# A four-layer graph stack: block sums copied by ScalarE in the third layer, projections taken before the factors

## The chip, the cores and the metric

The kernel runs on one core of a Trainium2 chip. The metric is device time in microseconds for one execution; the median of three executions is given for the kernel before. The core has a matrix engine (TensorE, PE in the profile; its weight loads are PEld), a vector engine (VectorE, DVE), an activation engine (ScalarE, ACT), a general engine (GpSimd, POOL) and a queue engine that issues transfers (SyncE, SP). Each takes its own instructions in order and waits for the others by semaphores. PE writes its products into PSUM, eight banks of 128 x 512 float32; all else is kept in SBUF. GpSimd works on SBUF only in this kernel.

## The reference

Four graph layers follow each other on x (4096 x 256, float32) with one adjacency matrix (4096 x 4096, integers). After each, the input is added and every row is normalised. The change touches the third layer and the start of the fourth:

```python
# layer 2 (the third)
h = x @ W
e = (h @ a[:D, 0])[:, None] + (h @ a[D:, 0])[None, :]
e = jnp.where(e > 0, e, NEG_SLOPE * e)
attention = jax.nn.softmax(jnp.where(adj > 0, e, MASK_VAL), axis=1)
x = _layernorm(x + jax.nn.elu(attention @ h))
...
# layer 3 (the fourth)
Qn, Kn = _cos_normalize(x @ Wq.T), _cos_normalize(x @ Wk.T)
att = jax.nn.softmax(jnp.where(adj > 0, Kn @ Qn.T, NEG), axis=1)
x = _layernorm(x + 0.5 * (att @ x) + 0.5 * x)      # rows without a neighbour keep x
```

The exponential of the third layer's leaky sum splits into a part by source and a part by target, so the attention weight is a maximum of two products of factors, times the mask.

## The kernel before

**Tiling.** Rows are cut into 8 blocks (b) of 512. Within a block the 4096 neighbours are taken in 16 units (g) of 256. The third layer is `additive_one`. For every unit `weights` loads a mask (L552, SP), has ScalarE write two tiles of factors `r` (L564, into two PSUM banks) and VectorE turn each into attention weights, `prob` (L565, which reads one `r` and the mask). For blocks after the first, the product is done with seven half-sized multiplications in place of eight: `mix_weights` makes four combined tiles, the first two in one VectorE instruction (L434), the others by GpSimd (L435, L436). `prob` and `mix` have four buffers each.

**Sums.** `sums` runs a unit's seven products (`product`, L444), which add into four banks, `acc` 0 to 3, over the whole block. There is one set of these banks. At the end of a block the four banks are joined into the tile `quarters`: ScalarE copies half a bank to `one` (L449), VectorE adds the rest in two parts, `first_half` (L450, L452, L453) and `second_half` (L457, L458). The first block uses two banks and needs copies only (L587 to L589).

**Order.** The loop runs over all 128 units of the layer with a lag of three: in one step it issues the weights of unit i and the sums of unit i - 3, and then one step of finishing the block before. The code fixes the order of PE, VectorE and ScalarE as written; GpSimd and the transfers are placed by the scheduler. In the text, g=5 means the step that issues the sums of unit 5, and with it the weights of unit 8. When g is 15, the sums and the joining are issued ahead of the weights.

**Finishing a block.** `finish` projects the joined sums of the block before (`project`, L594, in steps g = 1, 2, 4, 6, into two banks `g`), and takes each projection: `take` has VectorE make the reciprocal of the weights' sum (L600) and ScalarE make `e` and `h` from it (L602, L603). `add` (L611, L612, L154, L155 on VectorE) adds the input, in steps 3, 4, 6, 8. `dots` (L502 on VectorE) and `sources` (L515 and a transfer on ScalarE, with unit 8) prepare the next block's factors. Before, `dots` wrote its products into one of the buffers of `h`.

**The fourth layer's preparation.** From the third block on, `follow.prepare` works ahead for the fourth layer, one step at a time: transposes (L127), a transfer out, four transfers back, sixteen multiplications (L1059), squares (L1066), scaled rows (L1075), and a second turn by transposes and transfers. The fourth layer itself is `cosine_attention`: scores (L1115) into two banks `p` or, for some, into the banks `g`, exponentials (L1119), masks (L1127), and the same `product`. `tail` finishes the third layer's last block inside it.

**PSUM.** Each layer opens its pools in turn. The third has `r` (2 banks), `acc` (4), `g` (2), in this order. The fourth had `acc` (4), `p` (2), `g` (2), so `p` stood on the last two banks of the third layer's `acc`.

Of the kernel before, what the change touches and what calls it, by code (L numbers as in the profile page):

```python
# [9 lines left out]
FP = mybir.dt.float32  # L10
# [4 lines left out]
OP = mybir.AluOpType  # L15
AX = mybir.AxisListType
PSUM = bass.MemoryType.PSUM

P = 128
D = 256  # L20
KC = D // P
QB = 4
QW = QB * P
# [5 lines left out]
def kernel(  # L29
# [27 lines left out]
    nc = tc.nc  # L57
    N = x.shape[0]
    NT = N // P
    NB = N // QW  # L60

    def pool(stack, name, bufs, **kw):
        return stack.enter_context(tc.tile_pool(name=name, bufs=bufs, reuse_waits="tile", **kw))
# [4 lines left out]
    fin1 = ctx.enter_context(tc.tile_pool(name="fin1", bufs=1))  # L68
# [352 lines left out]
    NP = NT // 2  # L421
    HW = QW // 2
# [24 lines left out]
    def first_half(c, one, acc):  # L447

        nc.scalar.copy(one, acc[3][:, :HW])  # L449
        nc.vector.tensor_tensor(c[:, :2, :], one.unsqueeze(1).to_broadcast([P, 2, HW]),  # L450
                                acc[0].rearrange("p (h i) -> p h i", h=2), OP.add)
        nc.vector.tensor_tensor(c[:, 2, :], c[:, 1, :], acc[1][:, :HW], OP.add)  # L452
        nc.vector.tensor_tensor(c[:, 3, :], c[:, 2, :], acc[1][:, HW:], OP.add)  # L453

    def second_half(c, acc):

        nc.vector.tensor_tensor(c[:, 1:3, :], c[:, 1:3, :], acc[2][:, :HW].unsqueeze(1).to_broadcast([P, 2, HW]), OP.add)  # L457
        nc.vector.tensor_tensor(c[:, 1, :], c[:, 1, :], acc[2][:, HW:], OP.add)  # L458

    def quarters(c, k):  # L460

        lo = k % 2 * P
        return [c[:, q, lo:lo + P] for q in ((0, 3), (1, 2))[k // 2]]
# [61 lines left out]
    def additive_one(w_sb, ga, tail, op, follow):  # L525

        with ExitStack() as lay:
# [4 lines left out]
            sb = pool(lay, "gb_sb", 2)  # L532
# [9 lines left out]
            mixed, acc, prob, mix, mvs, roots, kept, drawn, ys, far_y = {}, {}, {}, {}, {}, {}, {}, {}, {}, {}  # L542
# [4 lines left out]
            def weights(b, g):  # L547
                if b == 0 and g < 2:
                    mask = ga.first_mask[:, 2 * g:2 * g + 2, :]
                else:  # L550
                    mask = mp.tile([P, 2, QW], I32, name="mask")
                    nc.sync.dma_start(mask, edges[:, 2 * g:2 * g + 2, b * QW:(b + 1) * QW])  # L552
                if b < NB - 1:
                    if 4 <= g < 4 + QB:
                        ga.dots((b + 1) * QB + g - 4, (0,), sb, "h")
                    elif g == 8:
                        ga.sources(b + 1)
                    elif g == 11:
                        ga.row(b + 1, nc.sync)
                z = prob[b, g] = zp.tile([P, 2, QW], FP, name="prob")  # L560
                for n in range(2):
                    j = 2 * g + n
                    r = pr.tile([P, QW], FP, name="r")
                    nc.scalar.activation(r, ga.row_of(b), AF.Relu, bias=ga.less[:, j:j + 1], scale=ga.dst[:, j:j + 1])  # L564
                    nc.vector.scalar_tensor_tensor(z[:, n, :], r, ga.own[:, j:j + 1], mask[:, n, :], OP.add, OP.mult)  # L565
                if b:
                    s = mix[b, g] = zp.tile([P, 4, HW], FP, name="mix")
                    mix_weights(s, z, nc.gpsimd)

            def sums(b, g):  # L570
                if g == 0:
                    acc[b] = [pa.tile([P, QW], FP, name=f"acc{n}") for n in range(4)]
                if b:
                    for n in range(7):
                        product(acc[b], prob[b, g], mix[b, g], mixed[g // 2][:, g % 2], g, n)
                else:
                    for j in range(2 * g, 2 * g + 2):
                        for c in range(KC):
                            nc.tensor.matmul(acc[b][c], X[:, j, c * P:(c + 1) * P], prob[b, g][:, j % 2, :],
                                             start=(j == 0), stop=(j == NT - 1))  # L580
                if g == NP - 1:
                    c = kept[b] = op.tile([P, 4, HW], FP, name="quarters")
                    if b:
                        first_half(c, op.tile([P, HW], FP, name="one"), acc[b])
                        second_half(c, acc[b])
                    else:
                        nc.scalar.copy(c[:, :2, :], acc[b][0].rearrange("p (h i) -> p h i", h=2))  # L587
                        nc.vector.tensor_copy(c[:, 3, :], acc[b][1][:, :HW])
                        nc.vector.tensor_copy(c[:, 2, :], acc[b][1][:, HW:])  # L589

            def project(bank, b, k):
                po = drawn[b, k] = bank()
# [3 lines left out]
            def take(sb, b, k):  # L596

                po = drawn[b, k]
                rden = fin.tile([P, 1], FP, name="rden1")
                nc.vector.reciprocal(rden, po[:, D:D + 1])  # L600
                e, h = drawn[b, k] = sb.tile([P, D], FP, name="e"), sb.tile([P, D], FP, name="h")
                nc.scalar.activation(e, po[:, :D], AF.Exp, scale=rden)  # L602
                nc.scalar.activation(h, po[:, :D], AF.Relu, scale=rden)  # L603
# [11 lines left out]
            def finish(b, g):  # L615


                if g in (1, 2, 4, 6):
                    project(bank, b, g // 2)
                if g in (2, 3, 5, 7):  # L620
                    take(sb, b, g // 2 if g > 2 else 0)
                if g in (3, 4, 6, 8):
                    add(b, g // 2 - 1)
                elif g == 10:
                    roots[b] = begin_root(mvs[b])
                elif g == 11:
                    v, r, n = roots[b]
                    end_root(v, r, n, nc.gpsimd)
                    nc.gpsimd.tensor_tensor(v, mvs[b][:, :, 0], r, OP.mult)
                    nc.gpsimd.tensor_scalar(v, v, -1.0, 1.0, OP.mult, OP.add)  # L630
                elif g in (12, 13):
                    v, r, _ = roots[b]
                    for k in (2 * g - 24, 2 * g - 23):
                        y = ys[b][:, k, :]
                        nc.scalar.activation(y, y, AF.Identity, bias=v[:, k:k + 1], scale=r[:, k:k + 1])
                elif g == 14:
                    if b < NB - 2:
                        far_y[b] = saved.tile([P, QB, D], FP, name=f"far_y{b}")
                        nc.scalar.dma_start(far_y[b], ys[b])
                    else:  # L640
                        nc.scalar.dma_start(X[:, b * QB:(b + 1) * QB, :D], ys[b])
# [5 lines left out]
            with tc.manual_schedule(engines=fixed):  # L647
                for i in range(len(units) + LAG):
                    b, g = units[i - LAG] if i >= LAG else (-1, 0)
                    if g == NP - 1:  # L650
                        sums(b, g)
                    if i < len(units):
                        weights(*units[i])
                    if b >= 0:
                        if g < NP - 1:
                            sums(b, g)
                        if b:
                            finish(b - 1, g)
                        else:
                            for _ in range(3 if g > 3 else 0):  # L660
                                next(before, None)
                            if g == 11:
                                follow.start()
                            elif g == 14:
                                follow.centre(bank())
                            if g % 2:
                                t = mixed[g // 2] = keep.tile([P, 2, 4, P], FP, name=f"mixed{g // 2}")
                                mix_features(t, g // 2)
                        if b > 1 and g in (2, 4, 6, 8, 9, 10, 11, 12, 13, 14, 15):
                            follow.prepare(bank, b - 2, 1, ys[b - 2])  # L670
                        if b == NB - 1 and g > 3 and g % 2 == 0:
                            q = g // 2 - 2
                            nc.scalar.dma_start(X[:, q * QB:(q + 1) * QB, :D], far_y[q])
                        if b == NB - 1 and g in (3, 5, 7):
                            follow.load_mask(0, (g - 3) // 2, prob[b, g][:, 0, :1])
# [411 lines left out]
    def cosine_attention(co, tail):  # L1087
# [4 lines left out]
        with ExitStack() as lay:  # L1092
# [4 lines left out]
            far = pool(lay, "co_turn_far", 2, space=bass.MemoryType.DRAM)  # L1097
            co.turning = pool(lay, "co_turn", 1), None, far

            pa = pool(lay, "co_pa", 1, space=PSUM)  # L1100
            pz = pool(lay, "co_pz", 2, space=PSUM)
            ps = pool(lay, "co_ps", 2, space=PSUM)
            ov = out.rearrange("(t p) d -> p t d", p=P)
            mixed, acc, prob, mix, y, back = {}, {}, {}, {}, {}, {}
# [257 lines left out]
```

## Time and profile before

| what | value |
|---|---|
| median of three executions | 2815.4 us (2812.61 to 2818.65) |
| execution profiled | 2813.03 us |
| its span | 2811.2 us, mean granted clock of TensorE 0.998 |
| PE busy | 2776.7 us, 99% of the span |
| DVE busy | 2285.6 us, 81% |
| ACT busy | 1694.8 us, 60% |
| POOL busy | 1049.9 us, 37% |

A busy share is the time in which at least one instruction of an engine was under way, over the span. Matmuls overlap, and their ends are modelled, so a PE that is busy throughout need not be at its peak.

By stages, the third layer's seven blocks that use `mix` lie between 1773 and 2172 us. In these 399.0 us PE is busy for 386.85, DVE for 328.96, ACT for 228.19 and POOL for 197.04. A block from the third on lasts about 58.2 us, from one joining of sums to the next.

How the views are read: the table of waits has a line for each pair of waiting group and releaser, with the total in us, the number of waits and the longest. The timeline has the start, the duration of the merged instructions, the engine, the line, the tiles, and in square brackets the idle time ahead of it and its releaser. The chain of waits follows the last instruction back, each time to what released it, and shows the pieces by start and length. A releaser is inferred: it is the semaphore event that came last, and may not be the one that mattered.

### The profile page before, as it was taken

What the parts mean: (1) busy time and instruction counts of PE and PEld (TensorE: products, weight loads), DVE (VectorE), ACT (ScalarE), POOL (GpSimd) and SP (SyncE); (2) the same over time, 40 slices, a digit from 0 to 9 for tenths busy, and PEclk for the clock granted to TensorE, in tenths of its full rate; (3) what the DMA queues carried; (4) which work ended last, traced back from release to release, by engine and by line L of the source; (5) the groups of instructions that cost most, each with busy time, mean ns of one, the idle gap of its engine ahead of it and who ended that gap; (6) DMA issues with size and microseconds to landing.
All of it is one profiled execution on the core that took longest, in us unless ns stands there. A gap on an engine that the chain in (4) does not pass through costs nothing. (4 is left out here: it accounts for less than half of the span.)

```text
span 2811.2 us, 50179 instructions
## 1 busy us (share of the span) xinstructions
PE 2776.7 (99%) x19449; PEld 1427.4 (51%) x19449; DVE 2285.6 (81%) x3048; ACT 1694.8 (60%) x2641; POOL 1049.9 (37%) x983
## 2 busy tenths in 40 slices
PE   9999999999999999999999999999999999999998
PEld 5333333333443333333333333788888777777776
DVE  8899999999677788887888888888887777667676
ACT  8899999999246666666666665555555422222222
POOL 0001001001039878778778782444445100000000
PEclk9999999999999999999999999999999999999999
DMA  7566766665439899898998988567777545445451
GB/s 208 110 136 136 140 146 138 134 136 106 87 94 193 185 187 189 188 191 183 195 184 187 193 182 190 161 195 196 193 186 228 112 75 81 77 68 83 76 77 36
DMA packets 275064, 411.91 MB, mean 147 GB/s; under 512 B 54809, under 2 KB 155657, under 8 KB 273930
## 3 DMA queue, kind: packets, MB, share of 16 engines
q0 software_dynamic: 104176, 182.74, 41.0%
q1 hardware_dynamic: 164136, 218.75, 26.2%
q10 hardware_dynamic: 6514, 7.23, 0.7%
q8 instruction: 152, 2.49, 0.4%
q14 instruction: 86, 0.70, 0.1%
HBM read 335.94 MB, written 39.40 MB: 134 GB/s over the span
## 5 line engine op out<-in xcount | busy, mean ns | idle before, releaser
L830 DVE TENSOR_TENSOR prob<-p,mask 128x1024 f32<-128x1024 f32 x512 | 620.0, 1222 | 167.5 <-ACT p L820 161.1
L820 ACT ACTIVATE p<-p,shift 128x1024 f32<-128x1024 f32 x512 | 555.6, 1088 | 318.5 <-PE p L818 318.5
L310 PE MATMUL acc<-prob,V 128*32 128x512 f32 x6144 | 664.0, 592 | 1.2 <-DVE prob L300 1.2
L297 ACT ACTIVATE prob<-row,dst 128x512 f32<-128x512 f32 x1020 | 635.1, 713 | 0.6
L300 DVE SCALAR_TENSOR_TENSOR prob<-prob,mask 128x2048 f32<-128x2048 f32 x256 | 580.2, 2284 | 25.8 <-ACT prob L297 25.2
L840 POOL TENSOR_TENSOR den<-den,prob 128x1024 f32<-128x1024 f32 x220 | 556.2, 2528 | 96.2 <-DVE prob L830 88.0
L818 PE MATMUL p<-qT,kT 64*64 64x512 f32 x4096 | 531.1, 590 | 1.3 <-DVE prob L830 1.3
L854 PE MATMUL acc<-prob,V 64*64 64x512 f32 x4096 | 529.8, 589 | 0.0
L310 PEld LDWEIGHTS acc<-prob,V 128*32 128x32 f32 x6144 | 197.3, 110 | 453.0 <-issue 431.3
L444 PE MATMUL acc<-mix,mixed 128*128 128x256 f32 x1440 | 390.1, 380 | 2.2 <-DVE quarters L458 1.2
L854 PEld LDWEIGHTS acc<-prob,V 64*64 64x64 f32 x4096 | 157.4, 133 | 282.1 <-issue 280.3
L818 PEld LDWEIGHTS p<-qT,kT 64*64 64x64 f32 x4096 | 154.3, 133 | 278.2 <-issue 256.7
L444 PEld LDWEIGHTS acc<-mix,mixed 128*128 128x128 f32 x1440 | 271.7, 190 | 44.9 <-PE acc L444 3.5
L90 POOL COPY tick<-prob 128x1 f32<-128x1 f32 x35 | 38.5, 1100 | 642.4 <-DVE prob L300 641.5
L1127 DVE TENSOR_TENSOR prob<-prob,mask 128x1024 f32<-128x1024 f32 x128 | 156.1, 1220 | 149.8 <-ACT prob L1119 148.0
L444 PE MATMUL acc<-prob,X 128*128 128x256 f32 x960 | 247.8, 380 | 9.0 <-DVE quarters L450 9.0
L846 POOL DMA_DIRECT2D den<-prob x240 | 226.0, 942 | 59.5 <-DVE prob L830 30.1
L1046 POOL DMA_DIRECT2D mask<-in_adjT x64 | 47.8, 747 | 510.5 <-DVE prob L1127 424.4
L565 DVE SCALAR_TENSOR_TENSOR prob<-r,own,mask 128x512 f32<-128x512 f32 x252 | 177.1, 743 | 64.9 <-POOL mix L436 21.3
L444 PEld LDWEIGHTS acc<-prob,X 128*128 128x128 f32 x960 | 181.7, 190 | 89.7 <-issue 56.0
L1119 ACT ACTIVATE prob<-p 128x512 f32<-128x512 f32 x144 | 86.1, 598 | 198.8 <-PE p L1115 197.1
L1119 ACT ACTIVATE prob<-g 128x512 f32<-128x512 f32 x112 | 66.8, 596 | 199.5 <-PE g L1115 199.5
(221 smaller groups left out, 2803.7 us busy)
## 6 DMA issues: line engine op xcount, KB each, us to landing
mask<-in_adjT SPq DMA_DIRECT2D x254, 512.0 KB
den<-prob POOLq DMA_DIRECT2D x240, 512.0 KB, 5.2
mask<-edges SPq DMA_DIRECT2D x512, 64.0 KB
mask<-in_adjT POOLq DMA_DIRECT2D x64, 512.0 KB, 5.7
edges<-in_adj POOLq DMA_DIRECT2D x32, 512.0 KB, 9.6
far<-squares SPq DMA_DIRECT2D x16, 512.0 KB
den<-prob SPq DMA_DIRECT2D x16, 512.0 KB
row<-far SPq DMA_DIRECT2D x7, 1024.0 KB
```

The source lines that it names most:

```text
L297: nc.scalar.activation(z[:, h, :], r, AF.Relu, bias=-1.0, scale=dst[:, j, h:h + 1])
L300: nc.vector.scalar_tensor_tensor(z, z, 1.0, mask[m][:, j % MJ, :].unsqueeze(1).to_broadcast([P, H, QW]), OP.add, OP.mult)
L310: nc.tensor.matmul(acc[b][h * G:(h + 1) * G, n, :], part, prob[b, j][:, h, :], start=(j == 0), stop=(j == NT - 1))
L444: nc.tensor.matmul(acc[at][:, half * HW:(half + 1) * HW], w, a, start=(g == 0 and half == 0), stop=(g == NP - 1), skip_group_check=True)
L565: nc.vector.scalar_tensor_tensor(z[:, n, :], r, ga.own[:, j:j + 1], mask[:, n, :], OP.add, OP.mult)
L818: nc.tensor.matmul(p[c * d:(c + 1) * d, r, :], kT[half, c, at:at + d], qT[half, c, cols], start=True, stop=True)
L820: nc.scalar.activation(p, p, AF.Exp, bias=shift)
L830: nc.vector.tensor_tensor(z, p, mask[m][:, j % MJ, :].unsqueeze(1).to_broadcast([P, KC, QW]), OP.mult)
L840: nc.gpsimd.tensor_tensor(to, to, flat, OP.add)
L846: nc.gpsimd.dma_start(to, flat, accum_op=OP.add)
L854: nc.tensor.matmul(acc[b][c][r * d:(r + 1) * d, :], V[half, j, r * d:(r + 1) * d], prob[b, j][half, r, :], start=(j == 0), stop=(j == NH - 1))
L1127: nc.vector.tensor_tensor(z, z, co.mask[b, 2 * g // MJ][:, lo:lo + 2, :], OP.mult)
```

## The change

The change has six parts.

- At the end of blocks 1 to 6, ScalarE copies `one` and then the three banks of sums into SBUF (`taken`): two go straight to `quarters`, the third to a tile `two`. VectorE adds them there, in place (`first_half_taken`, `second_half_taken`). The second half comes after the next unit's weights, as `later()`. The last block is joined as before.
- The first block's sums are copied by ScalarE alone.
- `take` is moved from `finish` to the head of a step, ahead of the weights.
- `dots` writes to a buffer of its own, `kept1`, in blocks after the first.
- `follow.prepare` takes its second and third steps at g = 3 and 5, not 4 and 6. These are the transfer out and the transfers back.
- In the fourth layer the pool of `p` is opened ahead of that of `acc`, so `p` lies on the banks that `r` had, and `acc` where `acc` was.

```diff
+    def taken(c, one, two, acc):
+
+        nc.scalar.copy(one, acc[3][:, :HW])
+        for n, sb in enumerate((c[:, :2, :], c[:, 2:, :], two)):
+            nc.scalar.copy(sb, acc[n].rearrange("p (h i) -> p h i", h=2))
+
+    def first_half_taken(c, one):
+        nc.vector.tensor_tensor(c[:, :2, :], one.unsqueeze(1).to_broadcast([P, 2, HW]), c[:, :2, :], OP.add)
+        for n in (2, 3):
+            nc.vector.tensor_tensor(c[:, n, :], c[:, n - 1, :], c[:, n, :], OP.add)
+
+    def second_half_taken(c, two):
+        nc.vector.tensor_tensor(c[:, 1:3, :], c[:, 1:3, :], two[:, 0, :].unsqueeze(1).to_broadcast([P, 2, HW]), OP.add)
+        nc.vector.tensor_tensor(c[:, 1, :], c[:, 1, :], two[:, 1, :], OP.add)
...
-                        ga.dots((b + 1) * QB + g - 4, (0,), sb, "h")
+                        ga.dots((b + 1) * QB + g - 4, (0,), *((fin1, "kept1") if b else (sb, "h")))
...
-                    if b:
-                        first_half(c, op.tile([P, HW], FP, name="one"), acc[b])
+                    one = op.tile([P, HW], FP, name="one")
+                    if b == NB - 1:
+                        first_half(c, one, acc[b])
                         second_half(c, acc[b])
+                    elif b:
+                        two = fin1.tile([P, QW], FP, name="kept0").rearrange("p (h i) -> p h i", h=2)
+                        taken(c, one, two, acc[b])
+                        first_half_taken(c, one)
+                        return lambda: second_half_taken(c, two)
                     else:
                         nc.scalar.copy(c[:, :2, :], acc[b][0].rearrange("p (h i) -> p h i", h=2))
-                        nc.vector.tensor_copy(c[:, 3, :], acc[b][1][:, :HW])
-                        nc.vector.tensor_copy(c[:, 2, :], acc[b][1][:, HW:])
+                        nc.scalar.copy(c[:, 3, :], acc[b][1][:, :HW])
+                        nc.scalar.copy(c[:, 2, :], acc[b][1][:, HW:])
+                return lambda: None
...
-                if g in (2, 3, 5, 7):
-                    take(sb, b, g // 2 if g > 2 else 0)
...
-                    if g == NP - 1:
-                        sums(b, g)
+                    later = sums(b, g) if g == NP - 1 else lambda: None
+                    if b > 0 and g in (2, 3, 5, 7):
+                        take(sb, b - 1, g // 2 if g > 2 else 0)
                     if i < len(units):
                         weights(*units[i])
+                    later()
...
-                        if b > 1 and g in (2, 4, 6, 8, 9, 10, 11, 12, 13, 14, 15):
+                        if b > 1 and g in (2, 3, 5, 8, 9, 10, 11, 12, 13, 14, 15):
                             follow.prepare(bank, b - 2, 1, ys[b - 2])
...
+            pz = pool(lay, "co_pz", 2, space=PSUM)
             pa = pool(lay, "co_pa", 1, space=PSUM)
-            pz = pool(lay, "co_pz", 2, space=PSUM)
```

## The prediction

> **What bounds the kernel now.** I read the page first. TensorE (PE) is busy 99% of the span, so the first idea is that the change can gain only what PE loses in waits. The table of PE's waits names the change's target: at the ends of the third layer's blocks PE waits for VectorE (DVE) to read the banks of sums. Six waits of up to 1.8 us and six of 0.2 us make 10.2 us in all.
>
> ```profile
> PE acc L444 <- DVE quarters L450: 9.0, 6, 1.8
> ...
> PE acc L444 <- DVE quarters L458: 1.2, 6, 0.2
> ```
>
> Next I asked whether PE sets the pace there or merely meets DVE once per block. The waits of DVE alone, over one block (1884.6 to 1942.9 us), are these, 9.1 us in all:
>
> ```profile
> DVE prob L565 <- POOL mix L436: 3.3, 2, 1.6
> DVE prob L565 <- ACT r L564: 2.3, 1, 2.3
> DVE prob L565 <- POOL s L167: 2.3, 1, 2.3
> DVE prob L565 <- POOL mix L435: 1.2, 1, 1.2
> ```
>
> None of them is for PE. The named releasers are the last semaphore seen; in the timeline each of these gaps ends 0.1 us after a ScalarE (ACT) factor, L564, has ended. In the whole layer DVE waits for PE only before L588, at its first block's end. So DVE and ACT together are a chain that paces itself at 58.2 us a block (L450 at 1883.89 and 1942.20), with DVE busy 48; PE has 55.6 us of work (58.2 less its 2.6 us of lost starts) and meets the chain at L450. Here is that meeting, on DVE's timeline: no gap ahead of L450, which is late because all before it is late.
>
> ```profile
> 1881.88 1.37 DVE L565 SCALAR_TENSOR_TENSOR prob<-r,own,mask 128x512 f32<-128x512 f32 x2
> 1883.28 0.69 DVE L434 TENSOR_TENSOR mix<-prob 128x512 f32<-128x512 f32 x1
> 1883.89 0.68 DVE L450 TENSOR_TENSOR quarters<-one,acc 128x512 f32<-128x512 f32 x1
> ```
>
> The chain that ended last confirms it. It leaves the layer through ACT and DVE and a transfer, not through PE:
>
> ```profile
> 2165.29 1.47 ACT r L564 x2
> ...
> 2169.60 1.30 DVE squares L127 x2
> ...
> 2171.20 5.46 DMA far<-squares
> ...
> 2176.69 0.71 DVE squares L127
> 2177.40 0.32 DVE quarters L453
> ```
>
> **What the skill says.** "Perfetto Trace Analysis", Identifying the Most-Contended Engine, calls matmul busy time a bad measure, since pipelined matmuls overlap. The trace agrees: PE is "99% busy" and still not what paces this layer. "SBUF — State Buffer", SBUF: two separate sides: a VectorE operation with two SBUF inputs and a GpSimd operation that reads SBUF lock each other out for a whole instruction. The trace agrees: L612 (two SBUF inputs, 256 wide) takes 0.83 us beside POOL's L435 and L436 and 0.42 us without, while L452 and L453, with one input in PSUM, take 0.42 us beside the same POOL work.
>
> **The change, part by part.** All is counted on the DVE/ACT chain, for PE has slack.
>
> *The sums by ScalarE.* A block's end now has ACT copy `one` (0.39 us, L449) and three banks (about 0.59 us each, as L587 shows), after L564 of the unit before. In the block above: 1881.5 to 1883.6 us, each bank free before PE needs it (1882.8, 1883.6 and 1884.5 us). So the waits on L450 and L458 do go. ACT's next L564 waited 3.4 us for DVE there, which hides the copies. DVE keeps five additions, 2.8 us a block (1883.89 to 1886.71), only now two SBUF inputs each. L434 (two SBUF inputs, 0.69) and L450 (0.68) show no gain from leaving PSUM; the lock can cost. POOL's L435 and L436 run beside them. Bounds 0 to 1.9 us a block end; I take 0.4 for each of two 256-wide additions and half of that for the third, 1.0. Six ends: +6.0 (0 to 11). The second half moved behind the next unit's weights brings that unit's `mix` 1.1 us forward, but lengthens nothing and shortens nothing in DVE's sum.
>
> *The takes moved ahead.* This is the large part. Here is what a take costs when nothing covers it (DVE, then ACT, block above, g=5):
>
> ```profile
> 1908.64 0.16 DVE L600 RECIPROCAL rden<-g 128x1 f32<-128x1 f32 x1
> 1910.43 1.41 DVE L565 SCALAR_TENSOR_TENSOR prob<-r,own,mask 128x512 f32<-128x512 f32 x2 [1.64 <-POOL mix L436]
> ```
>
> ```profile
> 1908.83 0.47 ACT L602 ACTIVATE e<-g,rden 128x256 f32<-128x256 f32 x1 [3.99 <-DVE rden L600]
> 1909.20 0.47 ACT L603 ACTIVATE h<-g,rden 128x256 f32<-128x256 f32 x1
> 1909.56 1.48 ACT L564 ACTIVATE r<-other_row,less,dst 128x512 f32<-128x512 f32 x2
> ```
>
> ACT takes its instructions in order, so the factors wait behind e and h, which wait for DVE's reciprocal: 1.79 us from reciprocal to the next L565. Today four takes a block stand at the end of a step. Those at g=5 and 7 are bare. Behind those at g=2 and 3, DVE has other work first: two transposes L127 (1.21) and a dot L502 (0.69), or an `add` (1.87). Put ahead of the step's weights, all four are bare but for one dot in two of them. The stretch from L434 of unit 4 to L565 of unit 6 lasted 4.98 us (1893.29 to 1898.27); it becomes 0.61 (rest of L434) + 1.79 + 2.05 (weights of unit 5) + 1.21 (transposes) + 1.79 = 7.45. One reciprocal (0.08) leaves the next stretch: +2.4. Takes at g=5 and 7 stay bare. But at g=5 `sources` (L515 and its DMA issue, 1902.69 to 1903.30) stood in the shadow of an `add`; now it stands between h and L564: +0.6. So blocks 2 to 6: 5 x 3.0 = 15.0. Block 1 prepares nothing; its first take is bare already (1785.42 to 1787.22): 1.80 - 0.34 (its dot) - 0.08 + 0.6 = 2.0. Block 7 has no dots and no sources: 2 x 1.71 = 3.4. Sum +20.4 (18 to 21).
>
> *First block's end.* DVE loses two copies (0.67), but ACT has two more (0.36 each) ahead of the L564 that DVE waits for: about +0.6.
>
> *Dots into kept1, transfers of `prepare` one step earlier.* No instruction more. SP issues `far` when the squares are there; mask loads queued behind have four buffers of lead. One mask wait of 2.5 us (L565 at 2151.95) might shrink. I count 0, and -2.5 to +2 in the range.
>
> *Score banks.* `p` now lies on the old factor banks and needn't wait for the second half (L458 ended at 2179.42, the first score began at 2179.52). Four scores took 5.46 us there, in starts 1.7 us of work, held by ACT's exponentials. Some can fill PE's 2.8 us wait for L453. Bounds 0 (the scheduler may keep the order) to -5; I take -3.
>
> Sum: 6.0 + 20.4 + 0.6 - 3 = +24.0. The chain into layer four goes through DVE, and from 2184.98 us on PE runs nearly without a gap (its waits after it are 1.3 us at most), so all of it reaches the end: 2813.0 (execution profiled; its span is 2811.2, with 1.8 around it) + 24.0 = 2837. The median shown is 2.4 above the profiled execution; I put 2838.
>
> **Rivals.** *PE is the bound* (ends faster). Place: the six block ends. Price: 10.2 us of waits gone, and 3 at the transition: 2813 - 13 = 2800 (2794 to 2807). For it: the 99% and the named waits. Against it: DVE is never held by PE. It would decide if DVE could run ahead in the freed time. *The takes cost nothing* (no change): the rotation only moves idle time, as if the gaps at g=2 and 3 came out of those at g=10 to 12 (2.3, 1.2 and 2.3 us). Then +6.6 at block ends and the first copy, less 2.6 us of lead that DVE keeps on PE at the last unit (L434 at 2167.59 + 1.55 for POOL, against PE's need at 2171.78), less 3: 2814 (2808 to 2821). Against it: those later gaps are ACT's own work, behind it in the same order, and start from DVE. *The lock at its worst and no gain at the transition*: 11 + 21 + 2.6 (copies and mask) = +35, 2848. *The banks' move does nothing*: 2840, within my range.
>
> **How the numbers follow.** A measurement here tells about 0.2%, 5.6 us, from no change. My forecast (2826 to 2846 as its own range) has 0.70, the worst lock 0.08, takes for nothing 0.10, PE as bound 0.12. Faster: 0.12 and 0.02 of the third case; within 0.2%: 0.07 of it; slower 0.79. The range runs from 2816 to 2849, leaving out the faster case and part of the middle one.
>
> **What would show it.** Right: PE's waits on L450 gone and new ones on `mix` (L434, L435) or `prob` in their place; blocks of some 62 us in layer three (58.2 + 3.0 + 1.0); DVE idle 1.2 to 1.7 us before L565 four times a block, not twice; L452 and L458's successors at up to 0.83 us. Wrong: blocks near 55.6 us with PE gapless, or DVE's idle time unchanged, or masks (L552) as the new releaser.

## The result, and the profile after

The changed kernel takes 2847.62 us (median of four executions, 2845.8 to 2849.25) beside 2814.01 (2810.21 to 2818.65) for the kernel before on the same chip. The ratio is 1.0119, with a 95% interval from 1.0107 to 1.0131: slower by 33.6 us. The span profiled is 2844.8 us, against 2811.2. The forecast was 2838, or 24 us more.

Line numbers move with the change: the factors L564 are L579 after it, `prob` L565 is L580, the masks L552 are L567, the reciprocal L600 is L622, `e` and `h` are L624 and L625, `src` L515 is L530, its transfer L517 is L532, the row load L523 is L538, scores L1115 are L1137, the projections L594 are L616, the preparation's products L1059 are L1081. ScalarE's copies at a block's end are L462 (`one`) and L464, VectorE's additions L467, L469, L472 and L473. L434 stays.

First the table of PE's waits in the third layer (1773 to 2215 us). Columns: the waiting group, its releaser, then total, number and longest.

```profile
PE acc L444 <- POOL mix L435: 10.6, 15, 0.9
PE acc L444 <- DVE squares L127: 10.3, 5, 2.3
PE acc L444 <- DVE prob L580: 7.6, 7, 1.6
PE g L616 <- DVE quarters L450: 2.0, 1, 2.0
PE g L616 <- DVE quarters L453: 0.4, 1, 0.4
```

The waits named for L450 and L458 at the banks of sums are gone, and the first three lines come to 28.5 us. But the name in the second line misleads. L127 writes nothing that L444 reads. All five of its waits end at the first product of a new block, 0.05 us after ScalarE's copy `one` (L462) has ended, and the weight load of the same product (PEld) names that copy:

```profile
1891.64 0.39 ACT L462 COPY one<-acc 128x256 f32<-128x256 f32 x1
1892.08 0.30 PEld L444 LDWEIGHTS acc<-prob,X 128*128 128x128 f32 x2 [1.80 <-ACT one L462]
1892.08 1.17 PE L444 MATMUL acc<-prob,X 128*128 128x256 f32 x4 [1.40 <-DVE squares L127]
```

So PE still waits at the banks of sums, 10.3 us in five of six block ends, against 10.2 before; only it waits for ScalarE now, not for DVE. On ScalarE the copies stand behind the factors. The other 18.2 us are new waits for the operands of its products, `mix` and `prob`.

The waits of DVE over one block (1894 to 1957.4 us) say where the pace is lost:

```profile
DVE prob L580 <- issue: 4.9, 3, 2.3
DVE prob L580 <- POOL mix L435: 2.5, 2, 1.3
DVE prob L580 <- ACT r L579: 2.3, 1, 2.3
DVE prob L580 <- POOL s L167: 2.3, 1, 2.3
DVE prob L580 <- DMA mask<-in_adjT: 1.3, 1, 1.3
```

The sum is 13.3 us, against 9.1 before: 4.2 more in a block. None of it is a wait for PE. "issue" means that the profile names no releaser. The timeline does: the four takes are in these lines, and three such gaps are listed in the next fence as seen by DVE, with what ScalarE did in the fence after it.

```profile
1906.40 1.41 DVE L580 SCALAR_TENSOR_TENSOR prob<-r,own,mask 128x512 f32<-128x512 f32 x2 [1.31 <-POOL mix L435]
...
1911.44 1.41 DVE L580 SCALAR_TENSOR_TENSOR prob<-r,own,mask 128x512 f32<-128x512 f32 x2 [0.94 <-issue]
...
1922.03 1.41 DVE L580 SCALAR_TENSOR_TENSOR prob<-r,own,mask 128x512 f32<-128x512 f32 x2 [2.28 <-issue]
```

```profile
1909.84 0.47 ACT L624 ACTIVATE e<-g,rden 128x256 f32<-128x256 f32 x1 [2.83 <-DVE rden L622]
1910.21 0.47 ACT L625 ACTIVATE h<-g,rden 128x256 f32<-128x256 f32 x1
1910.57 1.48 ACT L579 ACTIVATE r<-other_row,less,dst 128x512 f32<-128x512 f32 x2
```

The reciprocal at 1909.67 releases `e`; `h` follows, then the first factor (0.79 long, so its end is at 1911.36), and L580 starts at 1911.44. ScalarE had stood for 2.83 us, and the factors could have been made in that time had they not been queued behind `e`.

At a block's end, on DVE's timeline, the copies are in time for DVE, but two of the additions are dearer:

```profile
1894.02 0.69 DVE L467 TENSOR_TENSOR quarters<-one,quarters 128x512 f32<-128x512 f32 x1
1894.81 1.63 DVE L469 TENSOR_TENSOR quarters<-quarters 128x256 f32<-128x256 f32 x2
...
1898.41 0.69 DVE L472 TENSOR_TENSOR quarters<-quarters,kept 128x512 f32<-128x512 f32 x1
1899.13 0.42 DVE L473 TENSOR_TENSOR quarters<-quarters,kept 128x256 f32<-128x256 f32 x1
```

Last, the chain of waits at the layer's end. It leaves by the same transfer, only 33 us later than before (the transfer then began at 2171.20):

```profile
2198.61 1.38 ACT r L579 x2
...
2202.82 1.30 DVE squares L127 x2
2204.12 0.30 DVE mixed L427
2204.42 5.47 DMA far<-squares
...
2210.55 0.65 DVE quarters L450
```

To see where the time arises I compared the starts of all 112 executions of L434 in the seven blocks, after less before. The shift is +0.6 us ahead of the first block's end, and it grows by 4.5 us in block 1, 5.0 in each of blocks 2, 3 and 5, 5.7 in block 4, 4.7 in block 6 and 2.7 in block 7, to +33.2 us at the last L434. The end of the span is 33.7 later. So nearly all of the loss arises in the third layer.

### The profile page after: what moved, and what is told of

Its sections match the earlier page's. It is cut to its first block, busy times and chain, and to the rows that moved or that the text cites. A ratio compares the mean times of both kernels' runs of the same rounds, so it can differ in the third digit from the quotient of the medians.

```text
span 2844.8 us, 50175 instructions
## 1 busy us (share of the span) xinstructions
PE 2791.0 (98%) x19449; PEld 1431.4 (50%) x19449; DVE 2292.2 (81%) x3046; ACT 1703.1 (60%) x2661; POOL 1053.0 (37%) x983
## 5 line engine op out<-in xcount | busy, mean ns | idle before, releaser
L444 PE MATMUL acc<-mix,mixed 128*128 128x256 f32 x1440 | 396.1, 385 | 11.0 <-POOL mix L435 10.6
L444 PEld LDWEIGHTS acc<-mix,mixed 128*128 128x128 f32 x1440 | 274.7, 192 | 57.2 <-POOL mix L435 18.1
L444 PE MATMUL acc<-prob,X 128*128 128x256 f32 x960 | 251.6, 384 | 18.0 <-DVE squares L127 10.3
L580 DVE SCALAR_TENSOR_TENSOR prob<-r,own,mask 128x512 f32<-128x512 f32 x252 | 177.1, 743 | 93.2 <-issue 33.1
L444 PEld LDWEIGHTS acc<-prob,X 128*128 128x128 f32 x960 | 181.2, 191 | 105.0 <-issue 56.4
```

The costliest lines, as they stand in the source:

```text
L444: nc.tensor.matmul(acc[at][:, half * HW:(half + 1) * HW], w, a, start=(g == 0 and half == 0), stop=(g == NP - 1), skip_group_check=True)
```

## The experiments

**1. The takes back in their place.** The changed kernel without the move of `take`: the block ends, the banks and the steps of `prepare` stay changed.

```diff
-                    if b > 0 and g in (2, 3, 5, 7):
-                        take(sb, b - 1, g // 2 if g > 2 else 0)
...
+                if g in (2, 3, 5, 7):
+                    take(sb, b, g // 2 if g > 2 else 0)
```

> The changed kernel with the four takes of a block back at the end of their steps; all other parts of the change stay. Theory (VectorE and ScalarE pace the third layer, and the takes ahead of the factors are the cost): takes and the mask waits behind them go, about 28 us less than the changed kernel; left over is 0.6 us a block end for additions from SBUF and 0.8 us at the first block's end: 2818 us (2814 to 2823), blocks of 58.8 us. Rival (PE's waits at the block ends were the bound): these waits are gone here too, so 2800 us, blocks near 55.6 us.

Measured: 2820.41 us beside 2815.28, ratio 1.0019 (1.0011 to 1.0027). So all but the takes costs 5.1 us. In its trace the shift of L434 grows from 1.27 us in block 1's last unit to 5.39 at the last: 4.1 us for six block ends, 0.7 each. One trace gives this only roughly: in experiment 5, whose third layer is that of the kernel before, the same shift wanders by 1.8 us. Here PE's waits at the banks are really gone: it passes all six block ends without a gap. Nothing was gained by it, for PE now stands elsewhere, at the preparation's products, for ScalarE's `h`:

```profile
PE g L1081 <- ACT h L625: 11.2, 5, 3.0
```

**2. The takes alone.** The kernel before, with `take` moved ahead of the weights and with `kept1` for the dots.

> The kernel before with nothing but the takes moved ahead of the weights (and the dots' buffer that goes with them). Theory: +20 us of uncovered waits and +6 us of masks that come late: 2840 us (2836 to 2845), with 1.3, 0.9, 2.3 and 1.6 us idle ahead of L565 in a block, and a mask wait of 1 to 2 us near unit 12. Rival (the copies and additions at the block ends cost the time): 2814 to 2818 us.

Measured: 2843.1 us beside the same 2815.28, ratio 1.0104 (1.0089 to 1.0119), or 27.8 us more. The two halves add up: 5.1 + 27.8 = 32.9, against 33.6 for the whole change. But 27.8 is more than the 20.4 forecast for the takes. Its DVE waits hold four for masks, 4.3 us by name, in place of one of 2.5 us before:

```profile
DVE prob L565 <- DMA mask<-in_adjT: 4.3, 4, 1.4
```

**3. The masks: a first try.** In the changed kernel DVE waits for a mask near unit 12 of each block: 1.95, 1.09, 1.29, 1.72, 1.02 and 1.61 us in blocks 1 to 6, 8.7 in all (the first is named as a wait for PE in the table). Before, only block 1 had a gap there, of 0.35. In experiment 2 the six come to 5.7, two of them named as waits for PE. SyncE's timeline gives the reason. Here is a block of before, and then the same block after (the masks of the last line go on past the end of each view, at 1930 and 1940 us):

```profile
1904.01 0.39 SPq L552 DMA_DIRECT2D mask<-in_adjT  x1
1912.51 0.34 SPq L523 DMA_DIRECT2D first_row<-far  x1
1912.94 13.21 SPq L552 DMA_DIRECT2D mask<-in_adjT  x6
```

```profile
1917.12 0.39 SPq L567 DMA_DIRECT2D mask<-in_adjT  x1
1929.78 0.34 SPq L538 DMA_DIRECT2D first_row<-far  x1
1930.21 9.08 SPq L567 DMA_DIRECT2D mask<-in_adjT  x5
```

SyncE's queue has one row load among the masks. It must wait until the sources that ScalarE sends (L532, issued at 1920.74) have landed. The order on the queue is the same in both kernels. Yet after the change 12.7 us pass from the mask ahead of this load to the load itself, not 8.5, since the sources now go out later in relation to the masks ahead of them; the masks that follow leave in a burst, and the last of the burst comes too late for L580 at 1937.48. The Trainium skill ("DMA: Bandwidth & Descriptors", Anatomy of one DMA, a section on transfers that GpSimd issues) says that the DMA engines don't wait for semaphores and that the issuing sequencer does, before dispatch. The trace agrees for SyncE, which issues nothing for nearly all of those 12.7 us. From ScalarE's issue of the 2 KB of sources to the row load that waits for them it took 9.0 us.

I first moved the row load two steps later in the code:

```diff
-                    elif g == 11:
+                    elif g == 13:
                         ga.row(b + 1, nc.sync)
```

> The changed kernel with the load of the next block's row of sources issued with unit 13, not 11. Theory: SyncE stands at this load until the sources have landed, and the masks queued behind it come late; issued later, it no longer holds them, and the wait of 1.0 to 1.95 us at unit 12 goes in six blocks: 2839 us (2837 to 2842). Rival (masks are late because the transfers of prepare come a step earlier, or because the memory is busy): 2847 us, wait unchanged.

Measured: 2843.25 us beside 2815.28, ratio 1.0102 (1.0087 to 1.0117). The edit did not do what it was for. The scheduler places the transfers, and it put the load at the same place of SyncE's queue; in the trace every engine runs the same instructions in the same order as in the changed kernel. So the run says nothing about the theory, but it is a second measurement of the changed kernel: 28.0 us above the kernel before, where the first gave 33.6, and 5.1 us of mask waits near unit 12, where the first had 8.7. The loss is known no better than this, some 28 to 34 us.

**4. The row load on another queue.** Now the load goes out from ScalarE's queue, whose order the code fixes:

```diff
-                    elif g == 11:
-                        ga.row(b + 1, nc.sync)
+                    elif g == 13:
+                        ga.row(b + 1, nc.scalar)
```

> The changed kernel, but the row load that follows the sources goes out from ScalarE's queue at g=13 instead of SyncE's at g=11, so no mask load stands behind it. Theory: the mask waits at unit 12 (8.7 us in six blocks, of which some 1.6 to 2.5 are covered by other waits) come from SyncE standing at the row load; they go, and the time falls by 6 to 9 us against the changed kernel: about 2839 to 2842 beside 2814, ratio 1.009 to 1.010. Rival: the masks were a symptom, another wait (ACT r) takes their place: ratio stays at 1.012 and the gaps ahead of prob at unit 12 remain with another releaser. A second rival: ScalarE itself stands at the row load, and the time rises.

Measured: 2837.75 us beside 2813.91, ratio 1.0085 (1.0069 to 1.01). That is 23.8 us more than before instead of 33.6, and the intervals don't touch; beside the 28.0 of experiment 3 the gain is 4.2 us, and the intervals overlap. So it is worth 4 to 10 us, about what the mask waits near unit 12 came to in the two traces (5.1 and 8.7). In SyncE's timeline no row load stands among the masks, and of DVE's mask waits one is left:

```profile
1913.23 22.94 SPq L567 DMA_DIRECT2D mask<-in_adjT  x7
```

```profile
DVE prob L580 <- DMA mask<-in_adjT: 0.4, 1, 0.4
```

From one block to the next the shift of L434 now grows by 3.98, 3.99, 3.75, 3.85 and 3.17 us in blocks 2 to 6. The forecast had 3.0 for the takes and 1.0 for a block end. So the masks are what it left out.

Three rivals can be met from the traces. That the masks are late because `prepare` sends its transfers a step earlier does not fit: experiment 2 has those waits without that move, and experiment 1, with it, has none near unit 12. Nor was the memory busy: in the 8 us or so ahead of each of the six row loads of the changed kernel the DMA engines were 3 to 6% busy. And the mean granted clock from 1773 to 2172 us was 0.98 in the changed kernel and 1.00 here. But a slower PE could delay the layer only through waits of DVE and ScalarE for it. In the changed kernel DVE's list has one, which is the mask wait of block 1, and ScalarE's copies at the block ends have 0.3 us.

**5. The score banks alone.** The kernel before with only the order of the two pools exchanged.

> The kernel before with nothing changed but the two pools of the fourth layer exchanged, so that the score banks lie on the old factor banks. Theory (the transfer and VectorE's first half set the end of layer three, whatever the scores do): no change, 2813 to 2816 beside 2814, ratio 0.9995 to 1.0005. Rival (the forecast's step): some scores fill TensorE's wait, -3 us, ratio 0.999, down to -5.

Measured: 2813.62 us beside 2813.91, ratio 0.9997 (0.9988 to 1.0006). No gain is seen; the interval, -3.4 to +1.7 us, just leaves room for the forecast's 3. In this trace PE's wait of 2.8 us for L453 is no longer listed, since scores run there, and this one stands in its stead, for ScalarE's exponentials:

```profile
PE p L1115 <- ACT prob L1119: 2.4, 1, 2.4
```

**6. The fourth layer's preparation later.** In the changed kernel, a transpose L127 that waits 3.14 us for the transfer stands ahead of L450 on DVE (2209.92 and 2210.55 us); before, L450 came ahead of it. I moved the fourth layer's last two preparations:

```diff
-            steps = {(0, j + n): (NB - 2 + b, step) for b, j in enumerate((1, 12)) for n, step in ((0, 3), (4, 3), (5, 1), (7, 1), (8, 3))}
+            steps = {(0, j + n): (NB - 2 + b, step) for b, j in enumerate((5, 14)) for n, step in ((0, 3), (4, 3), (5, 1), (7, 1), (8, 3))}
```

> The changed kernel with the fourth layer's last two preparation chains four and two steps later (5 and 14 for 1 and 12), so that the squares which wait for a transfer need not stand ahead of the last block's joining of sums on VectorE. Theory: the whole first half stood 3.1 us behind that transfer at 2209.92, and this is what ate the gain forecast for the score banks: -2 to -5 us against the changed kernel, ratio about 1.0105. Rival: the joining is followed by the same chain (weights of the fourth layer, its transfer) later, so the same time is lost there: ratio 1.012.

Measured: 2846.22 us beside 2816.07, ratio 1.0108 (1.0091 to 1.0125). The interval holds both the theory's 1.0105 and the rival's 1.012, so this is inconclusive. The trace speaks for a partial trade: PE waits 3.7 us for the transfer, at the preparation's own products, where it waited 0.4.

```profile
PE g L1081 <- DMA xT<-far: 3.7, 1, 3.7
```

**7. The take split in two.** If it is the order on ScalarE that costs, then the reciprocal may come early as long as `e` and `h` stand behind the factors. In the changed kernel the reciprocal goes back to the end of the step, and `e` and `h` follow in the next step, behind its factors and just ahead of `add`. `take` now makes the reciprocal alone, `take_rest` makes `e` and `h`:

```diff
+                if g in (3, 4, 6, 8):
+                    take_rest(sb, b, g // 2 - 1)
                 if g in (2, 3, 5, 7):
-                    take(sb, b, g // 2 if g > 2 else 0)
+                    take(b, g // 2 if g > 2 else 0)
```

> The changed kernel with each take cut in two: the reciprocal at the end of its old step, e and h on ScalarE behind the next step's factors, just ahead of the addition that needs them. The work is the same. Theory (the cost is the order: factors behind e and h behind the reciprocal): the four waits of a block go (6.1 us in the changed kernel, 3.3 in the kernel before), the VectorE chain falls to about 55 us a block, level with PE: 2800 us (2796 to 2806), faster than both. Rival 1 (ScalarE's work as such is the cost): 2835 to 2848 us. Rival 2 (e and h later hold the two projection banks, and PE waits for those): 2808 to 2820 us, with PE waits at L1081 or L616.

Measured: 2804.69 us beside 2815.28, ratio 0.9964 (0.995 to 0.9978). It is faster than both kernels. On DVE's timeline a reciprocal is followed by L580 without a gap:

```profile
1907.03 0.16 DVE L621 RECIPROCAL rden<-g 128x1 f32<-128x1 f32 x1
1907.10 1.39 DVE L580 SCALAR_TENSOR_TENSOR prob<-r,own,mask 128x512 f32<-128x512 f32 x2
```

for on ScalarE's the factor stands ahead of `e`, and was done by then:

```profile
1905.76 1.48 ACT L579 ACTIVATE r<-other_row,less,dst 128x512 f32<-128x512 f32 x2 [2.52 <-DVE prob L580]
1907.22 0.47 ACT L627 ACTIVATE e<-g,rden 128x256 f32<-128x256 f32 x1
```

**8. Both, the split take and the row load on ScalarE's queue.**

> The split take (reciprocal at the end of a step, e and h behind the next step's factors) together with the row load on ScalarE's queue at g=13. Theory: the two waits are separate, so the mask waits left in the split kernel (about 4 us) go as well: 2798 to 2803 beside 2814, ratio about 0.995. Rival: with the takes out of the way the sources come earlier and the masks were no longer late enough to matter: the same as the split kernel alone, ratio 0.9964.

Measured: 2805.76 us beside 2816.07, ratio 0.9965 (0.9952 to 0.9978). This is a miss for the theory: there is no gain over the split alone. With the load off SyncE's queue DVE waits for masks as long as without: 12.7 us in five waits, against 11.2 in eight, and in each kernel the largest of them (7.0 and 5.5 us) lies in block 7, which prepares no next block and so loads no row. With the sources earlier again the row load was no longer what made masks late. For block 7 SyncE's timeline shows a like pattern: in the split kernel it issues nothing from 2123.28 to 2130.42 us, then the four transfers back (L135), which need the transfer out, and then the masks behind them. Whether this is the cause was not tried.

**9 and 10. The split take on the kernel before,** without ScalarE's copies, without and with the row load moved.

> The kernel before with the split take alone (reciprocal at the end of a step, e and h behind the next step's factors; the dots' products in a buffer of their own). Block ends stay with VectorE reading the banks, prepare's steps and the score banks as before. It tells whether ScalarE's copies are worth anything once VectorE and ScalarE are shorter. Theory A (that chain still paces): the split kernel less the copies' +5.3 us, so 2798 to 2801 beside 2814, ratio 0.995. Theory B (with the chain some 15 us shorter TensorE paces, and the waits at the banks of sums, 10.2 us before, are now its own): 2804 to 2809, ratio 0.997 to 0.998, with PE <- DVE L450 still at some 6 to 10 us.

> The same, with the row load on ScalarE's queue at g=13. If mask waits cost time in that kernel: 1 to 4 us less than the split take on the kernel before; if TensorE paces (theory B): no change against it, 0.997 to 0.998.

Measured: 2803.09 us beside 2814.37, ratio 0.9961 (0.9946 to 0.9976), and 2803.13, ratio 0.9957 (0.994 to 0.9974). All four split kernels are the same within their intervals, so ScalarE's copies are worth nothing here either. Theory B is right that TensorE sets the pace by then: a block lasts 56.1 us (L450 at 1881.75, 1937.89, 1994.11, 2050.26), close to the 55.6 of PE's own work, and DVE is now held by PE, which in the kernel before it was at the first block's end alone:

```profile
DVE prob L565 <- PE acc L444: 5.4, 4, 2.2
```

It is wrong in its signature: PE's products no longer wait for L450, although DVE still reads the banks itself. All its listed waits for DVE are these, the first of them at the layer's end:

```profile
PE g L594 <- DVE quarters L453: 3.3, 1, 3.3
PE acc L444 <- DVE quarters L458: 1.0, 5, 0.2
```

So these waits, the aim of the copies, were only the place where a late DVE met PE. With DVE early they vanish without a copy.

## Why the prediction was right, and where it was not

*What paces the layer.* Right. The waits at the banks left in experiment 1 and no time with them, and they vanished in experiment 9, where the order on ScalarE was changed (and the dots' buffer with it). Each time it was the ScalarE and VectorE chain that moved the end. One step failed without cost: "each bank free before PE needs it". In the changed kernel `one` came 1.4 to 2.3 us late for PE in five of six blocks, because PE, ahead of the slower chain, reaches the new block first.

*The takes (+20.4).* Right in mechanism and in size, once the masks are set apart. The stretch of four takes shows idle times of 1.31, 0.94, 2.28 and 1.64 us ahead of L580, four bare takes where there were two. With the row load on its own queue the five blocks that have all the costs grew by 3.75 us on average, against 4.0 forecast for takes and block end together. Experiment 2, the takes alone, gave 27.8, of which 5.7 are mask waits.

*The block ends (+6.0).* Right in sign, large by a third: 4.1 us in experiment 1. Two 256-wide additions take 1.63 us (L469), 0.8 more than two of 0.42, and that was forecast at 0.4 each. "SBUF — State Buffer", SBUF: two separate sides, gives the lock with GpSimd as the reason, and the third addition (L473), forecast at 0.2 more, speaks for it within one trace. In the changed kernel it took 0.42 in the four ends where no addition of POOL ran beside it, and 0.83 and 1.26 in the two where L435 did. In experiment 1 L435 ran beside all six, and it took 0.83 to 1.23. No run took POOL's work away, and why an end costs less than its additions there (0.7) was not tried.

*Masks (0, with -2.5 to +2).* This step failed, and "masks (L552) as the new releaser", which stood among the signs of being wrong, came. It said "mask loads queued behind have four buffers of lead" and looked at the transfers of `prepare` alone. Blocks 1 to 6 waited 8.7 us for masks (5.1 in experiment 3), because the sources, which moved with the takes, release a row load in the middle of SyncE's queue. The step had counted `sources` at 0.6 us a block for its place on ScalarE, but not followed its transfer to who waits for it. Taking the load off that queue gave back 9.8 us (33.6 less 23.8), or 4.2 beside experiment 3.

*Score banks (-3).* Not seen: 0.3 us in experiment 5, and in the changed kernel the shift from the last L434 to the end of the span is +0.4. In the changed kernel scores did run on PE from 2205.57 us on, while it waited for the sums, but the fourth layer's start still hangs on DVE, ScalarE and the transfer. Whether a small gain is hidden in the changed kernel by the order of L127 and L450 stays open, since experiment 6 didn't settle it.

*The sum.* 20.4 + 6.0 + 0.6 - 3 gave 24.0, and 2838. The first measurement, 2847.6, lies outside the forecast's own range of 2826 to 2846, the second, 2843.3, inside it. For the profiled pair the parts are 19.8 for takes + 4.1 for ends + 0.8 for the first block's end + 8.0 for masks + 0.4 at the transition + 0.6 ahead of the layer = 33.7, the difference of the spans. Here 8.0 is the difference of the L434 shifts of the changed kernel and of experiment 4, each less its shift at the layer's start (32.6 - 24.6), and 19.8 is what is left of 24.6 for the takes after the two other terms. Each part is from single traces, and good to 1 or 2 us. That the takes come so near to 20.4 is in part luck.

*The rivals.* "PE is the bound" said 2800 with the block ends as its place. It falls for this change. But its number is near the floor that the split kernels reach, 2803 to 2806, where TensorE does pace the layer. "The takes cost nothing" falls by experiment 2. "No gain at the transition, and masks" gave 2848, nearly the time of the first measurement, for half the right reasons: its masks and copies were 2.6 us, and the worst lock, 11, did not come.

## What to carry to other kernels

Where two engines feed each other in order, look at what stands ahead of the operation that the other one waits for. Here the changed kernel takes 2847.6 us with `e` and `h` ahead of the factors and 2804.7 with them behind, a difference that includes the mask waits which the first order set off. Removing the named waits of the busiest engine was worth nothing. When a step with a transfer is moved, follow the transfer to the load that waits for it, and then to all that is queued behind that load. A wait at which the slower partner merely arrives late goes away for good when that partner is made faster; removed in another way, it turned up at another place (experiment 1). And before a wait is called gone, see what runs where it stood: in the changed kernel it was there under another name.

## What the runs showed of the hardware

A transfer of 2 KB, sources from 128 partitions of four numbers, let the load that waits for it go 9.0 to 11.2 us after ScalarE issued it, in blocks 1 to 6 of the changed kernel. In the last 8 us or so of each such time the DMA engines were only 3 to 6% busy. And DVE's two additions of 256 elements took 0.82 us each beside POOL's work, and 0.42 when one operand lay in PSUM; an addition of the same size with both operands in SBUF took 0.42 when POOL was not adding. To read sums from SBUF in place of PSUM was no gain for VectorE.
